# Attention with image prompts on one core: who sums the products of the last batch, and in which order its closing work runs

## The chip, the core and the metric

The kernel runs on one NeuronCore of a Trainium2 chip. A core has a matrix engine (PE, with weight loads shown apart as PEld), a vector engine (DVE), a scalar engine (ACT), a general engine (POOL, GpSimd) and a queue for transfers (SP). Each engine works through its own instructions in order and waits on semaphores for the others. The metric is the device time of one execution in microseconds (us). Three executions of the kernel before took 462.03, 462.84 and 463.11 us: a median of 462.84.

## What is computed

Eight batches (B) of 112 queries (S) with 320 channels, 20 heads of 16 channels, attend to 375 rows of context of width 512: 371 text rows and four image-prompt rows. The shapes of the inputs and the part of the reference that matters:

```python
q = heads(hidden_states @ W_q)
k_t = heads(text_ehs @ W_k)
v_t = heads(text_ehs @ W_v)
scores_t = jnp.einsum('bhsd,bhtd->bhst', q, k_t) * attn_scale
probs_t = jax.nn.softmax(scores_t, axis=-1)
text_out = jnp.einsum('bhst,bhtd->bhsd', probs_t, v_t)
k_ip = heads(ip_ehs @ W_k_ip)
v_ip = heads(ip_ehs @ W_v_ip)
attn_scores = jnp.einsum('bhsd,bhnd->bhsn', q, k_ip) * attn_scale
qsem = jnp.einsum('bhst,bte->bhse', probs_t, text_ehs)
qsem = _l2norm(qsem)
ip_n = _l2norm(ip_ehs)
sem = jnp.einsum('bhse,bne->bhsn', qsem, ip_n)
fused = attn_scores + SEM_SCALE * sem
probs_ip = jax.nn.softmax(fused, axis=-1)
probs_ip = probs_ip * spatial_mask[None, None, :, None]
ip_out = jnp.einsum('bhsn,bhnd->bhsd', probs_ip, v_ip)
out = text_out + IP_SCALE * ip_out
out = out @ W_out + b_out
out = out + residual
```

The norm of `qsem` needs, for every query and head, p G p', where p is a row of probabilities and G is the matrix of inner products of the text rows. The kernel computes it so, without forming `qsem`.

## The kernel before

All data are float32. The 20 heads of a batch go in five groups of four (`GROUP`, `NG`); a step (b, g) is one group of one batch, and 40 steps make the kernel. Batches are numbered 0 to 7, so "batch 7" is the last one and "the sixth" is b = 6.

**A step.** `scores` (L529 on, matmul L540) multiplies queries and keys of one head into a PSUM bank; `probabilities` takes the row maximum on DVE (L553), the exponential on ACT (L557) and sends the row by SP into a ring of two tiles (L560). This is done two steps ahead (`LEAD`). `transposed` turns the four heads' probabilities on DVE (L568). `multiplied` is the *product*: 96 matmuls on PE (L587) of the transposed probabilities with the tile `u`, which holds one triangle of G (off-diagonal parts doubled), the inner products with the four prompts, a column of ones and the values. Each of the four heads writes a bank of its own. `value_sums` copies the last 21 columns of each bank on ACT (L600). `reduced` multiplies the first 371 columns by the probabilities and sums them on DVE (L606) into `ss`; when the DVE and ACT have read a bank, the next product may write it. `placed` copies the next group's values into `u` on POOL (L506): three copies, each of which must wait until the running product has read that part of `u`.

**Banks.** PSUM has eight: four for the products (`ps_qd`), two for scores (`ps_sc`), two for everything else (`ps_mm`). In the last step of all, heads 0 and 1 use `ps_mm` banks.

**`finish(b)`** is a generator of pieces, each run by one call of `run(("f", b), ...)` or `next`: F1 (L640 to L647: `xb` on POOL, `z`, `rn` on DVE), F2 (L650: square root on ACT with a table load for it, then a table load for Exp; the scaled values `attn` on POOL, L656), F3 (L661 to L667: five small DVE operations up to `fu`), F4 (L671: Exp on ACT), F5 (L677 to L692: four small DVE operations up to `w`; then on POOL the product of prompt values and weights, L684, and three sums, L690 to L692), F6 (transposes on PE, L698; copy on ACT, L702), F7 (projection by `wo_sb` on PE, L711, six matmuls; bias and residual on DVE, L718) and F8 (the output's transfer on SP). In the last batch `finish` runs twice, once for heads 0 to 15 (`first`) and once for heads 16 to 19 (`last`, on DVE in place of POOL).

**Order.** PE, SP, DVE and ACT run in the order in which the code issues. POOL is ordered by the framework's planner, from a model of the times. In batches 0 to 6 `between(b, g)` puts the work for batch b + 1 between products: G in g = 0, `values` in g = 1 and 2, `keys` in g = 2 and 3. The keys come in three chunks of 128 channels; the last chunk holds 64 channels (heads 16 to 19) with gaps. For batches after the first its numbers are taken out of `values`: the weights `wv_sb` carry 64 more columns, the product is 384 wide in place of 320, POOL copies the additional columns to `k3` (L474), and PE transposes them (L439) in g = 3.

In the last batch nothing follows, so PE has only the five products, their scores, and what is left of `finish(6)` and `finish(7)`. Pieces of `finish(6)` lie so: F1 after product 0, F2 within product 1, F3 and F4 after it, F5 ahead of product 2, F6 after product 3, F7 and F8 among the first pieces of `first`. `awake` issues idle matmuls of the identity (L371).

Of the kernel before, what the change touches and what calls it, by code (L numbers as in the profile page):

```python
# [8 lines left out]
F32 = mybir.dt.float32  # L9
AF = mybir.ActivationFunctionType  # L10
ALU = mybir.AluOpType
# [9 lines left out]
def kernel(  # L21
# [60 lines left out]
    def bank(name, spare=False):  # L82

        if spare:
            return ps_sc.tile([P, 512], F32, tag="sc", name=name)
        return ps_mm.tile([P, 512], F32, tag="mm", name=name)
# [344 lines left out]
    def keys(b):  # L431
        s = st[b]
        for i in range(NC):
            ps = bank(f"ps_k_{b}_{i}")
            if b > 0 and i == FULL:

                for c in range(NT):
                    rows = min(P, TT - c * P)
                    nc.tensor.transpose(  # L439
                        ps[:, c * P : c * P + rows],  # L440
                        s["k3"][:rows, c].rearrange("p a r d -> p (a r d)"),
                        ident[:rows, :rows],
                    )
                nc.scalar.copy(s["kT"][:, i, :], ps[:, :TT])
                yield
                return
            for e in range(NE):
                nc.tensor.matmul(  # L448
                    ps[:, :TT],
                    wk_sb[:, e, i * P : (i + 1) * P],  # L450
                    s["ctxT"][:, e, :TT],
                    start=(e == 0),
                    stop=(e == NE - 1),
                )
            nc.scalar.copy(s["kT"][:, i, :], ps[:, :TT])  # L455
            yield

    def values(b):
        s = st[b]
        ctxT, vext = s["ctxT"], s["vext"]  # L460
        w = C if b == 0 else C + REST
        for c in range(NT):
            ps = bank(f"ps_v_{b}_{c}")
            for e in range(NE):
                nc.tensor.matmul(  # L465
                    ps[:, :w],
                    ctxT[:, e, c * P : (c + 1) * P],
                    wv_sb[:, e, :w],
                    start=(e == 0),
                    stop=(e == NE - 1),  # L470
                )
            nc.scalar.copy(vext[:, c, :w], ps[:, :w])  # L472
            if b > 0 and c == NT - 1:
                nc.gpsimd.tensor_copy(  # L474
                    s["k3"][:, :, :, 0, :],
                    vext[:, :, C:].rearrange("p c (a d) -> p c a d", d=D),
                )
            yield
# [31 lines left out]
    def prompt_logits(b):  # L510
        s = st[b]
        qT, _, j = queries[b]
        ps = bank(f"ps_ip_{b}")
        for i in range(NC):
            heads = slice(0, HC, 1) if i < FULL else slice(0, HC, 2)
            hn = min(HC, H - i * HC)
            nc.tensor.matmul(  # L517
                ps[:S, i * HC * NIP : (i * HC + hn) * NIP],
                qT[:, i, j * S : (j + 1) * S],
                kipb[:, i, b, heads, :],  # L520
                start=True,
                stop=True,
            )
        nc.scalar.copy(s["ipl"], ps[:S, :HN].rearrange("p (h n) -> p h n", n=NIP))
        yield
# [48 lines left out]
    def multiplied(b, g):  # L574
        s = st[b]
        xT = s.pop(("xT", g))
        banks = []
        for a in range(GROUP):

            if (b, g) == steps[-1] and a < 2:  # L580
                banks.append(bank(f"ps_qd_{b}_{g}_{a}"))
            else:
                banks.append(ps_qd.tile([P, 512], F32, tag="qd", name=f"ps_qd_{b}_{g}_{a}"))
        for j in range(BLK):
            c, q = j // QN, j % QN
            for a in range(GROUP):
                nc.tensor.matmul(  # L587
                    banks[a][:S, j * RG : UW],
                    xT[a * RG : (a + 1) * RG, j, :S],
                    region(b, c)[a * RG : (a + 1) * RG, q, q * RG :],  # L590
                    start=(j == 0),
                    stop=(j == BLK - 1),
                )
            yield
        s["qd", g] = banks
# [3 lines left out]
        for h, ps in zip(groups[g], s["qd", g]):  # L599
            nc.scalar.copy(s["pvs"][:, h, :], ps[:S, TT:UW])  # L600

    def reduced(b, g):
        s = st[b]
        for a, (h, ps) in enumerate(zip(groups[g], s.pop(("qd", g)))):
            junk = small.tile([S, TT], F32, tag="junk", name=f"junk_{b}_{h}", bufs=1)
            nc.vector.tensor_tensor_reduce(  # L606
                out=junk,
                in0=ps[:S, :TT],
                in1=s["p", g][:, a, :],
                scale=1.0,  # L610
                scalar=0.0,
                op0=ALU.mult,
                op1=ALU.add,
                accum_out=s["ss"][:, h : h + 1],
            )
        del s["p", g]


    def finish(b, heads=(0, H), eng=None, late=False, table=None):
# [14 lines left out]
        def over_ip(t):  # L634
            return t.unsqueeze(2).to_broadcast([S, n, NIP])
# [41 lines left out]
        nc.vector.tensor_reduce(sx, ex, AX.X, ALU.add)  # L677
        rx = sm("rx")
        nc.vector.reciprocal(rx, sx)
        nc.vector.tensor_scalar_mul(rx, rx, sm_sb)  # L680
        w = sm4("w")
        nc.vector.tensor_tensor(w, ex, over_ip(rx), ALU.mult)  # L682
        wv = work.tile([S, NIP, H, D], F32, tag="wv", name=f"wv_{b}_{h0}", bufs=1)[:, :, :n]
        eng.tensor_tensor(  # L684
            wv,
# [1 line left out]
            w.rearrange("p h n -> p n h").unsqueeze(3).to_broadcast([S, NIP, n, D]),  # L687
            ALU.mult,
        )
        eng.tensor_tensor(wv[:, :2], wv[:, :2], wv[:, 2:], ALU.add)  # L690
        eng.tensor_tensor(ah, ah, wv[:, 0], ALU.add)
        eng.tensor_tensor(ah, ah, wv[:, 1], ALU.add)  # L692
        yield

        i0, i1 = h0 * D // P, -(-h1 * D // P)
# [18 lines left out]
        if h1 < H:  # L714
            yield
            return
        ob = work.tile([S, C], F32, tag="ob", name=f"ob_{b}", bufs=1)
        nc.vector.tensor_tensor(ob, ps[:S, :C], s["xb"], ALU.add)  # L718
        yield
# [16 lines left out]
    def run(key, make, pieces=1):  # L736

        if key not in gens:
            gens[key] = make()
        for _ in range(pieces):  # L740
            next(gens[key], None)

    def between(b, g):
# [26 lines left out]
        if g == 3:  # L770
            if new:
                run(("k", nb), None, 1)
            for bs in first if b > 0 else ():
                run(("q", bs[0]), lambda: project_queries(bs), 3)
            run(("t", b), lambda: prompt_logits(b))
            if new:
                run(("k", nb), None, 1)
            if b > 0 and new:
                run(("f", b - 1), None)
            for bs in rest:  # L780
                run(("q", bs[0]), None)
        if g == 4:
            if nb + 1 < B:
                run(("c", nb + 1), lambda: transposed_context(nb + 1))
            if b > 0 and new:
                run(("f", b - 1), None)
            if nb + 1 < B:
                run(("c", nb + 1), None, 2)
            for bs in (first if b > 0 else []) + rest:
                run(("q", bs[0]), None)  # L790
# [87 lines left out]

    b = B - 1
    before = ("f", b - 1)
    for g in range(NG):
        coming = g + LEAD if g + LEAD < NG else None
        for a in (2, 3, 0, 1) if coming and g > 0 else ():
            scores(b, coming, a)
            probabilities(b, coming, a)
        if g == 2:
            run(before, None)
        for j, _ in enumerate(multiplied(b, g)):  # L890
            for a in {0: (2, 3), 1: (0, 1)}.get(j, ()) if g == 0 else ():
                scores(b, coming, a)
                probabilities(b, coming, a)
            if j == 2 and g + 1 < NG:
                transposed(b, g + 1)
            if j == 2 and g == 1:
                run(before, None)
        if g == 0:
            run(("f", b - 2), None)
        value_sums(b, g)  # L900
        reduced(b, g)
        if g + 1 < NG:
            placed(b, g + 1)
        if g == 1:
            prompt_values(b)
        between(b, g)
        if g == 1:
            run(before, None, 2)
        if g == 2:
            nc.scalar.preload_act_table(AF.Sqrt)  # L910
        if g == 3:
            run(before, None)

            first = finish(b, (0, FULL * HC), table=AF.Sqrt)
            for _ in range(4):
                next(first)
            run(before, None)
            next(first)
            run(before, None)
    last = finish(b, (FULL * HC, H), nc.vector, late=True)  # L920
    awake(16, end=True)
    for _ in range(4):
        next(last)
    next(first)
    next(first)
    drain(first)
    awake(3, end=True)
    drain(last)


# [41 lines left out]
```

## Time and profile before

| what | us |
|---|---|
| median of three executions | 462.84 |
| the profiled execution | 463.68 |
| its span, first to last instruction | 461.9 |
| PE busy / PEld busy | 444.7 / 341.1 |
| DVE busy | 317.0 |
| ACT busy | 183.7 |
| POOL busy | 108.0 |
| batch 6 (351 to 402): PE busy of 51.00 | 50.86 |
| batch 7 and the end (402 to 462): PE busy of 60.00 | 47.56 |

An engine's busy time is what its instructions took; a matmul that waits for a bank inside a pipelined run is still shown as busy, so a full PE row does not mean that it computes all the time. A row of the timeline gives start, duration, engine, line, operation, written and read tiles, shape, count, and in square brackets the idle time of the engine before it with what ended it. The granted clock of PE (PEclk) is 1.00 or 0.50, and stretches that mix the two lie between.

### The profile page before, as it was taken

The numbers are of one execution on the slowest core, as the hardware profiler recorded it, in microseconds if no ns is written. First come the engines' busy times: TensorE is split into PE (matmuls) and PEld (weight loads), VectorE is DVE, ScalarE is ACT, GpSimd is POOL, SyncE is SP. The second block draws the span as 40 slices with busy tenths as digits, with TensorE's granted clock in tenths as the row PEclk, the third lists the DMA queues.
The fourth block names the chain that finished last, engine by engine and source line by source line (L and its number), as shares of the span: only waits on it lengthen the run. The fifth ranks groups of instructions, "written<-read, shape, count | busy, mean of one in ns | idle before, by whom it ended". The sixth has DMA issues, their size and how long they took to land.

```text
span 461.9 us, 12998 instructions
## 1 busy us (share of the span) xinstructions
PE 444.7 (96%) x5147; PEld 341.1 (74%) x5147; DVE 317.0 (69%) x692; ACT 183.7 (40%) x505; POOL 108.0 (23%) x257
## 2 busy tenths in 40 slices
PE   8998999999999999999999999999999999999595
PEld 8757867787678877777678876787678877867373
DVE  3047466786768768786768768786768768798664
ACT  2263233345344443435344443435334434335131
POOL 4302200102051115111051115121051115011541
PEclk9999999999999999999999999999999999989798
DMA  8669954645655464546654464546654364544100
GB/s 254 168 163 255 201 156 108 152 125 160 164 137 132 141 170 129 131 128 174 166 134 130 144 170 128 128 134 173 170 133 125 86 175 121 132 139 124 44 14 12
DMA packets 52068, 64.99 MB, mean 141 GB/s; under 512 B 18368, under 2 KB 43984, under 8 KB 52008
## 3 DMA queue, kind: packets, MB, share of 16 engines
q1 hardware_dynamic: 51568, 63.62, 52.1%
q8 instruction: 40, 0.66, 0.6%
q10 hardware_dynamic: 440, 0.56, 0.4%
q14 instruction: 20, 0.16, 0.1%
HBM read 19.46 MB, written 5.12 MB: 53 GB/s over the span
## 4 chain that ended last, share of the span: by engine, by line
PE 91%; DVE 3%; ACT 2%; POOL 1%; DMA 1%; issue 1%; DVEq 0%
PE ps_qd L587 42%; PE ps_v L465 14%; PE ps_k L448 10%; PE ps_g L412 8%; PE ps_s L540 4%; PE ps_o L711 3%; PE ps_q L301 3%; PE ps_c L351 2%; PE ps_g L384 1%; DVE junk L606 1%; PE ps_k L439 1%; PE ps_ip L517 1%; ACT kT L455 1%; DVE xgT L568 1%; DMA ct<-in_ctx_dram 1%
## 5 line engine op out<-in xcount | busy, mean ns | idle before, releaser
L587 PE MATMUL ps_qd<-u,xgT 32*112 32x104 f32 (+11 forms) x3840 | 223.7, 357 | 7.5 <-POOL u L506 6.8
L587 PEld LDWEIGHTS ps_qd<-u,xgT 32*112 32x112 f32 x3840 | 185.5, 174 | 48.5 <-issue 11.9
L553 DVE TENSOR_REDUCE nmx<-ps_s 112x1 f32<-112x371 f32 x160 | 77.6, 529 | 70.0 <-PE ps_s L540 69.4
L568 DVE STREAM_TRANSPOSE xgT<-xg 128x1536 f32<-128x1536 f32 x40 | 118.8, 2970 | 5.5 <-DMA xg<-p 5.5
L557 ACT ACTIVATE p<-ps_s,nmx 112x371 f32<-112x371 f32 x160 | 82.5, 572 | 60.6 <-DVE nmx L553 51.1
L606 DVE CUSTOM_DVE_ANT_0 junk<-ps_qd,p 112x371 f32<-112x371 f32 x160 | 86.8, 542 | 25.5 <-ACT pvs L600 8.2
L506 POOL COPY u<-vr 128x64 f32<-128x64 f32 x120 | 26.0, 240 | 171.6 <-PE ps_qd L587 115.9
L465 PE MATMUL ps_v<-wv_sb,ctxT 128*128 128x384 f32 (+1 forms) x192 | 64.7, 487 | 0.0
L540 PE MATMUL ps_s<-kT,qm 32*112 32x371 f32 x320 | 63.0, 478 | 0.4 <-ACT p L557 0.4
L465 PEld LDWEIGHTS ps_v<-wv_sb,ctxT 128*128 128x128 f32 x192 | 35.2, 190 | 20.8
L600 ACT COPY pvs<-ps_qd 112x21 f32<-112x21 f32 x160 | 16.5, 189 | 80.2 <-PE ps_qd L587 80.1
L448 PE MATMUL ps_k<-ctxT,wk_sb 128*128 128x371 f32 x136 | 45.9, 482 | 0.0
L412 PE MATMUL ps_g<-ctxT 128*128 128x375 f32 (+2 forms) x168 | 37.4, 379 | 0.0
L448 PEld LDWEIGHTS ps_k<-ctxT,wk_sb 128*128 128x128 f32 x136 | 25.1, 190 | 15.4 <-issue 0.5
L412 PEld LDWEIGHTS ps_g<-ctxT 128*128 128x128 f32 x168 | 28.1, 190 | 8.4
L540 PEld LDWEIGHTS ps_s<-kT,qm 32*112 32x112 f32 x320 | 25.4, 170 | 4.6 <-ACT kT L455 2.0
L310 DVE TENSOR_SCALAR qm<-ps_q,emask 128x224 f32<-128x224 f32 (+1 forms) x25 | 9.2, 400 | 25.4 <-PE ps_q L301 25.4
L684 POOL TENSOR_TENSOR wv<-vip,w 112x1280 f32<-112x1280 f32 (+1 forms) x8 | 19.3, 2408 | 19.6 <-DVE w L682 19.6
L472 ACT COPY vext<-ps_v 128x384 f32<-128x384 f32 (+1 forms) x24 | 11.3, 472 | 27.5 <-PE ps_v L465 26.9
L455 ACT COPY kT<-ps_k 128x371 f32<-128x371 f32 x17 | 8.0, 469 | 27.5 <-PE ps_k L448 27.5
L400 ACT ACTIVATE ug<-ps_g 128x375 f32<-128x375 f32 (+2 forms) x24 | 9.0, 377 | 23.5 <-PE ps_g L412 20.5
L401 POOL TENSOR_TENSOR ug<-ug,half 128x128 f32<-128x128 f32 (+1 forms) x24 | 10.9, 457 | 29.9 <-ACT ug L400 29.9
(109 smaller groups left out, 317.3 us busy)
## 6 DMA issues: line engine op xcount, KB each, us to landing
xg<-p SPq DMA_DIRECT2D x160, 162.3 KB
u<-ug SPq DMA_DIRECT2D x128, 99.0 KB
vip<-vipd SPq DMA_DIRECT2D x8, 560.0 KB
ct<-in_ctx_dram SPq DMA_DIRECT2D x16, 256.0 KB
vr<-vd SPq DMA_DIRECT2D x32, 120.0 KB
vd<-vext SPq DMA_DIRECT2D x7, 320.0 KB
ct<-in_ctx_dram SPq DMA_DIRECT2D x8, 224.0 KB
vd<-vext SPq DMA_DIRECT2D x7, 160.0 KB
```

The costliest lines, as they stand in the source:

```text
L412: nc.tensor.matmul(ps[:, : T - t0], ctxT[:, e, t0 : t0 + P], ctxT[:, e, t0:T], start=(e == 0), stop=(e == NE - 1),)
L448: nc.tensor.matmul(ps[:, :TT], wk_sb[:, e, i * P : (i + 1) * P], s["ctxT"][:, e, :TT], start=(e == 0), stop=(e == NE - 1),)
L465: nc.tensor.matmul(ps[:, :w], ctxT[:, e, c * P : (c + 1) * P], wv_sb[:, e, :w], start=(e == 0), stop=(e == NE - 1),)
L506: nc.gpsimd.tensor_copy(region(b, c)[:, :, UV - c * P :], s["vr"][:, c * QN : (c + 1) * QN, g, :])
L540: nc.tensor.matmul(ps[:S, :TT], qm[a * RG : (a + 1) * RG, i, r, j * S : (j + 1) * S], s["kT"][a * RG : (a + 1) * RG, i, :], start=True, st ...
L553: nc.vector.tensor_reduce(nmx, ps[:S, :TT], AX.X, ALU.max, negate=True)
L557: nc.scalar.activation(p, ps[:S, :TT], AF.Exp, bias=nmx)
L568: nc.vector.transpose(xT.rearrange("p j (k q) -> p q j k", q=QN), xg.rearrange("p q (j k) -> p q j k", k=RG),)
L587: nc.tensor.matmul(banks[a][:S, j * RG : UW], xT[a * RG : (a + 1) * RG, j, :S], region(b, c)[a * RG : (a + 1) * RG, q, q * RG :], start=(j ...
L600: nc.scalar.copy(s["pvs"][:, h, :], ps[:S, TT:UW])
L606: nc.vector.tensor_tensor_reduce(out=junk, in0=ps[:S, :TT], in1=s["p", g][:, a, :], scale=1.0, scalar=0.0, op0=ALU.mult, op1=ALU.add, accu ...
L684: eng.tensor_tensor(wv, s["vip"][:, :, part], w.rearrange("p h n -> p n h").unsqueeze(3).to_broadcast([S, NIP, n, D]), ALU.mult,)
```

## The change

1. The square sums of heads 0 and 1 of steps g = 0, 1 and 2 of the last batch leave DVE. A new generator `shared` copies both banks to SBUF on ACT, multiplies by the probabilities on POOL, and sums with an accumulating ACT instruction that is issued in the following step (`drain(sums)`, ahead of the product). DVE's `reduced` starts at head 2 there.
2. The third chunk of the last batch's keys is made by a product of its own (four matmuls, each recorded as two) after product 1. The last batch's `values` are 320 wide, the copy to `k3` and the transposes in (6, 3) go.
3. Pieces of `finish(6)`: F2, F3 and F4 within product 1; F5 after product 2 (it was ahead of it); F6 and the projection after product 4 (they were ahead of it). F7 is split: the projection, then the addition of bias and residual, then the transfer.
4. Banks: in step 3 heads 0 and 1, in step 4 heads 2 and 3 use `ps_mm`. The last batch's prompt logits use a score bank.
5. The Sqrt table for the end is loaded ahead of product 3 and no longer after product 2. `first` runs five pieces in a row after product 3.
6. In F5 one DVE operation goes (the mask is folded into the one that follows), and `last` sums the prompts by one reduction and one addition in place of three additions. `awake` has 14 and 2 rounds in place of 16 and 3 (a round is two recorded matmuls).

```diff
-            if b > 0 and i == FULL:
+            if 0 < b < B - 1 and i == FULL:
...
-        w = C if b == 0 else C + REST
+        w = C + REST if 0 < b < B - 1 else C
...
-            if b > 0 and c == NT - 1:
+            if w > C and c == NT - 1:
...
-        ps = bank(f"ps_ip_{b}")
+        ps = bank(f"ps_ip_{b}", spare=b == B - 1)
...
-            if (b, g) == steps[-1] and a < 2:
+            if b == B - 1 and (g, a // 2) in ((NG - 2, 0), (NG - 1, 1)):
                 banks.append(bank(f"ps_qd_{b}_{g}_{a}"))
...
-    def reduced(b, g):
-        s = st[b]
-        for a, (h, ps) in enumerate(zip(groups[g], s.pop(("qd", g)))):
+    def shared(b, g):
+
+        s = st[b]
+        some = list(enumerate(zip(groups[g], s["qd", g])))[:2]
+        t = work.tile([P, NE, TP], F32, tag="ctxT", name=f"shared_{b}_{g}")
+        prods = [t[:S, a, :TT] for a, _ in some]
+        p = s["p", g]
+        for a, (h, ps) in some:
+            nc.scalar.copy(prods[a], ps[:S, :TT])
+        yield
+
+        for a, _ in some:
+            nc.gpsimd.tensor_tensor(prods[a], prods[a], p[:, a, :], ALU.mult)
+        yield
+
+        for a, (h, _) in some:
+            nc.scalar.activation(prods[a], prods[a], AF.Copy, accum_out=s["ss"][:, h : h + 1])
+        yield
+
+    def reduced(b, g, a0=0):
+        s = st[b]
+        for a, (h, ps) in list(enumerate(zip(groups[g], s.pop(("qd", g)))))[a0:]:
...
-        nc.vector.tensor_scalar_mul(rx, rx, sm_sb)
         w = sm4("w")
-        nc.vector.tensor_tensor(w, ex, over_ip(rx), ALU.mult)
+        nc.vector.scalar_tensor_tensor(w, ex, sm_sb, over_ip(rx), ALU.mult, ALU.mult)
...
-        eng.tensor_tensor(wv[:, :2], wv[:, :2], wv[:, 2:], ALU.add)
-        eng.tensor_tensor(ah, ah, wv[:, 0], ALU.add)
-        eng.tensor_tensor(ah, ah, wv[:, 1], ALU.add)
+        if late:
+            ips = small.tile([S, GROUP, D], F32, tag="ips", name=f"ips_{b}", bufs=1)
+            nc.vector.tensor_reduce(ips, wv.rearrange("p n h d -> p h d n"), AX.X, ALU.add)
+            nc.vector.tensor_tensor(ah, ah, ips, ALU.add)
+        else:
+            eng.tensor_tensor(wv[:, :2], wv[:, :2], wv[:, 2:], ALU.add)
+            eng.tensor_tensor(ah, ah, wv[:, 0], ALU.add)
+            eng.tensor_tensor(ah, ah, wv[:, 1], ALU.add)
...
         if h1 < H:
             yield
             return
+        yield
+
         ob = work.tile([S, C], F32, tag="ob", name=f"ob_{b}", bufs=1)
...
-            if new:
+            if nb < B - 1:
                 run(("k", nb), None, 1)
...
             if b > 0 and new:
-                run(("f", b - 1), None)
+                run(("f", b - 1), None, 2)
...
     before = ("f", b - 1)
+    sums = iter(())
     for g in range(NG):
...
-        if g == 2:
-            run(before, None)
+        drain(sums)
+        if g == 3:
+            nc.scalar.preload_act_table(AF.Sqrt)
...
             if j == 2 and g == 1:
-                run(before, None)
+                run(before, None, 3)
+        value_sums(b, g)
+        if g < LEAD + 1:
+            sums = shared(b, g)
+            next(sums)
+            reduced(b, g, 2)
+        else:
+            reduced(b, g)
+        if g + 1 < NG:
+            placed(b, g + 1)
+        if g < LEAD + 1:
+            next(sums)
         if g == 0:
             run(("f", b - 2), None)
-        value_sums(b, g)
-        reduced(b, g)
-        if g + 1 < NG:
-            placed(b, g + 1)
         if g == 1:
             prompt_values(b)
+            run(("k", b), None)
         between(b, g)
-        if g == 1:
-            run(before, None, 2)
         if g == 2:
-            nc.scalar.preload_act_table(AF.Sqrt)
+            run(before, None)
         if g == 3:
-            run(before, None)
 
             first = finish(b, (0, FULL * HC), table=AF.Sqrt)
-            for _ in range(4):
+            for _ in range(5):
                 next(first)
-            run(before, None)
-            next(first)
-            run(before, None)
     last = finish(b, (FULL * HC, H), nc.vector, late=True)
-    awake(16, end=True)
-    for _ in range(4):
+    run(before, None, 2)
+    awake(14, end=True)
+    for _ in range(3):
         next(last)
+    run(before, None)
+    next(last)
     next(first)
     next(first)
+    run(before, None)
     drain(first)
-    awake(3, end=True)
+    awake(2, end=True)
     drain(last)
```

## The prediction, made before the changed kernel was run

> **What bounds the kernel now.** I read the page first: PE is busy 444.7 of 461.9 us, and up to 403 us its row has no hole, so there only PE's own work counts. Then the timeline of each engine over batch 7. There PE waits ahead of every product. The products' rows:
>
> ```profile
> 411.14 8.20 PE L587 MATMUL ps_qd<-u,xgT 32*112 32x392 f32 x93 [0.58 <-DVE ss L606]
> 420.40 6.78 PE L587 MATMUL ps_qd<-u,xgT 32*112 32x392 f32 x96
> 432.78 6.96 PE L587 MATMUL ps_qd<-u,xgT 32*112 32x392 f32 x96 [5.60 <-POOL u L506]
> 443.09 4.80 PE L587 MATMUL ps_qd<-u,xgT 32*112 32x392 f32 x96
> ```
>
> The same 96 matmuls take 4.80 us in product 4 and up to 8.20 elsewhere. In 1 and 2 the first four matmuls wait one by one for DVE's sums to free the banks: by the weight loads, all four are free at 413.13 and 422.39. Product 3 waits 5.6 us for POOL, whose queue is this:
>
> ```profile
> 426.58 2.47 POOL L684 TENSOR_TENSOR wv<-vip,w 112x1280 f32<-112x1280 f32 x1 [6.61 <-DVE w L682]
> 429.13 1.54 POOL L690 TENSOR_TENSOR wv<-wv 112x640 f32<-112x640 f32 x1
> 430.75 0.86 POOL L691 TENSOR_TENSOR attn<-attn,wv 112x320 f32<-112x320 f32 x1
> 431.68 0.86 POOL L692 TENSOR_TENSOR attn<-attn,wv 112x320 f32<-112x320 f32 x1
> 432.49 0.58 POOL L506 COPY u<-vr 128x64 f32<-128x64 f32 x3
> ```
>
> The rest is the clock. Stretches of 3.41 us, laid so that every change of the granted clock falls on an edge (columns: PE, PEld, DVE, ACT and POOL busy, PEclk, DMA share, GB/s):
>
> ```profile
> 409.89:413.30 3.41, 2.83 (x18) 1.02 (x15) 2.94 (x11) 0.32 (x4) 0.24 (x1) 1.00 0.51 145
> 413.30:416.71 3.41, 3.41 (x28) 2.65 (x30) 3.38 (x7) 2.56 (x5) 0.00 (x0) 0.50 0.12 30
> 420.13:423.54 3.41, 3.31 (x25) 1.66 (x26) 2.84 (x13) 0.00 (x0) 0.00 (x0) 1.00 0.40 129
> 423.54:426.95 3.41, 3.41 (x80) 3.28 (x74) 3.23 (x10) 2.23 (x5) 0.36 (x1) 1.00 0.17 45
> 426.95:430.37 3.42, 0.23 (x3) 0.11 (x2) 3.28 (x4) 1.70 (x5) 3.34 (x2) 1.00 0.54 152
> 430.37:433.78 3.41, 1.00 (x8) 0.68 (x12) 3.12 (x7) 0.00 (x0) 2.54 (x6) 0.50 0.00 0
> ```
>
> A stretch with 1.02 us of weight loads is followed by half clock, one with 1.66 is not. So PE need not be idle for a whole stretch: losing about half of one suffices, and costs 1.7 us (half of the next).
>
> **The changes, in the trace's own clock.** *Batch 6.* `values` at 384 columns: 16 matmuls in 5.36 us in the chain of waits, 0.335 each; at 320, estimated in proportion, 0.279. 24 matmuls save 1.34. The three transposes save 0.51 (chain, 394.20). PE is the bound there (50.86 of 51.00 busy) and the next products' banks and `u` are ready 0.9 us or more before PE comes, so all **1.85** counts.
>
> *Product 1.* DVE comes late to the sums of product 0 (410.45, after its transpose) and needs 0.70 for each head. New: after `value_sums` (ends 410.21) ACT copies heads 0 and 1; the nearest row, the copy of `kT` (371 columns, 469 ns), gives 410.68 and 411.10. DVE's two heads end at 411.75. Product 1 then runs from 411.75 instead of 413.13 with only 1.2 us lost, so with no cold stretch, and ends at 416.45 (4.7 us, as product 2 from 422.39) instead of 419.6. That is 3.1 us, and ACT gives most of it back. ACT's queue before:
>
> ```profile
> 414.13 1.95 ACT L557 ACTIVATE p<-ps_s,nmx 112x371 f32<-112x371 f32 x4 [3.92 <-DVE nmx L553]
> 416.10 1.28 ACT L650 ACT_TABLE_LOAD   x1
> 417.40 0.22 ACT L650 ACTIVATE rn<-rn 112x20 f32<-112x20 f32 x1
> 417.63 1.28 ACT L651 ACT_TABLE_LOAD   x1
> 419.49 0.41 ACT L600 COPY pvs<-ps_qd 112x21 f32<-112x21 f32 x4 [0.57 <-PE ps_qd L587]
> ```
>
> The exponentials end 1.39 earlier (two heads fewer on DVE): 414.69. Then come two accumulating ACT instructions, an operation that this trace does not have. Bounds: 0.4 (the copy alone) and 1.0 each (twice the exponential's 0.49); I take 0.52, by the exponential's row. 415.75. Two table loads and the root: 418.53; F3 on DVE, 1.37 after the root (its five operations, 422.26 to 423.63): 418.64; Exp 0.27: 418.93. Only now `value_sums` of product 1, 419.34, two copies, 420.25, the new `kT` copy, 420.70. Meanwhile PE does the own product of the keys, 8 recorded matmuls by the 2.7 us that 8 such took at 390.86: 416.45 to 419.15, **hidden** in PE's wait for ACT (without that cover it would cost 2.7). Scores of step 4 (8 in 1.1 us) then run 420.75 to 421.85, and product 2 starts: 421.85 against 422.39. It ends at 426.6 against 427.1.
>
> Behind the accumulating instructions stand, on ACT, the table loads and all of the above: each additional 0.1 us of one costs 0.2 here. In steps 2 and 3 ACT has 1.9 and 0.8 us of slack ahead of `value_sums`.
>
> *Product 3.* F5 now comes after `placed(3)`. Banks of heads 0 and 1 are the free `ps_mm` ones; those of 2 and 3 need ACT's copies: 426.6 + 0.1 + 0.41 + 2 x 0.45 = 428.0. `u` is complete at 427.2, the transposed tile (DVE, scores at 421 on, four maxima, 2.9) at 426. Start 428.0 in place of 432.78, warm (1.1 us lost): end **432.8** in place of 439.67.
>
> *Product 4.* What is late next is POOL again, one step on. It multiplies heads 0 and 1: width 371 lies between the rows 112x320 (0.86) and 112x640 (1.55), so 0.97 each, 427.55 to 429.5. Then F5's chain; its `w` is ready at 429.15 (DVE: two heads to 428.3, three small operations). 5.95 us as above: 435.45. `placed(4)` follows, by the order that POOL kept before (426.58 to 432.49): 436.05. Banks are free by 435.0, the logits end at 433.55, F6 and F7 no longer stand here (2.4 us with their wait). Start 436.1 in place of 443.09. But PE has then been idle 2.5 us, and most positions of a 3.41 us stretch hold enough of that: 1.6 us of cold clock. End 436.1 + 4.8 + 1.6 = **442.5** against 447.93, which is 5.4 earlier.
>
> *The end,* counted from product 4's. Before: 461.9 - 447.93 = 13.97. New, on PE: transposes, `value_sums` and copy 1.0; projection 1.87, now here; 28 idle matmuls at 0.12, 3.36; two transposes 0.4, ACT's copy 0.35, projection 4 x 0.31 now warm, 4 idle ones 0.48: 8.73. DVE's chain for the last four heads is ready at 7.4 (7.85 before, less 0.34 for the dropped operation and 0.1 for the reduction) and waits for PE. Transpose, copy, two matmuls, addition, transfer as before but warm: 1.65 + 2.98. Sum 13.36, so 0.6 better. DVE's addition for batch 6 fits into the 0.5 us in which DVE waits for Exp; POOL's `xb` has 3 us.
>
> **Sum:** 1.85 + 5.4 + 0.6 = 7.9 us of the span of 461.9. The profiled execution took 463.68, 0.8 over the median; the gain is taken off the median: 462.84 - 7.9 = **454.9, say 455.0**.
>
> **Two rules against the rows.** The Trainium skill, "TensorE: Matmul & The Clock Gate", section "HAM oscillation", warns of idle gaps beyond about 3.4 us. By it the 2.5 us ahead of product 4 would be free and the time 453.4; the row 409.89 (clock halved after a stretch that PE still worked in) says otherwise and I follow it. The 3.41 us spacing itself agrees with that page. "GPSIMD Engine Reference", section "Engine selection", advises VectorE over GpSimd for elementwise work, about twice as slow with two inputs. By it the move loses: 0.70 on DVE becomes 0.45 + 0.97 + 0.52 on two engines. Three steps, if all stood on the path, would lose 6 x 1.24 = 7.4 us. In the rows the bank is free after the first 0.45, and the other parts find POOL and ACT idle except where I charged them.
>
> **Rivals.**
> (a) Cold also at product 2. PE waits 1.65 us there before the scores; a stretch that holds all of it is on the edge between the two rows. Another 1.7: 456.7. 22%.
> (b) No cold stretch at product 4: the window falls well (453.4), or the planner puts `placed(4)` ahead of F5's chain, so that the product starts at 434.4 (451.7). Against it: POOL took the chain first before. 24%.
> (c) The planner puts the two POOL multiplications of step 2 behind F5's chain. They end at 437.05, ACT's sums, the Sqrt load and `value_sums` follow to 439.8, DVE's two heads to 441.0; product 4 starts there, cold: 460.1. Against it: the copies are ready before `w`. 7%.
> (d) Slower: the accumulating instruction is dear. Six of them stand in ACT's queue in steps 1 to 3, with 1.9 and 0.8 us of slack. At x us each the loss is 6(x - 0.52) - 2.7, and equals the whole gain at x = 2.3; at 3.0 the time is 467. No row is near such a price. 3%.
>
> My forecast has 40%; 4% is left for what I do not see. The range 451.2 to 458.2 takes in (a), (b) and accumulating instructions at their upper bound (1 us on top of (a)), and leaves out (c) and (d). A difference under 0.2% (0.9 us) cannot be told from none with runs that lie 1.1 us apart. Faster 95%, no change 2%, slower 3%.
>
> **What would show it.** Product 1 about 4.7 us long, with no half clock behind product 0; ACT's `value_sums` of product 1 idle-free behind Exp of F4; product 3 about 1.4 us after product 2; product 4 waiting for POOL's L506 behind F5's sums; half clock in it; and PE, not DVE, last at the end. I am wrong if ACT's sums exceed 1 us, if POOL's order differs, or if batch 6 does not shorten by 1.85.

## The result, and the profile after

The changed kernel takes 456.19 us (median of four, 455.51 to 457.10) against 462.98 for the kernel before on the same chip: a ratio of 0.9857, interval 0.983 to 0.9883. 455.0 was forecast. The profiled execution took 457.10 us, with a span of 455.3.

The four executions come in two pairs, 455.51 and 455.67 at a mean granted clock of 0.996 and 0.995, 456.71 and 457.10 at 0.991. One stretch of 3.41 us at half clock lowers the mean over 455 us by 3.41 / 2 / 455 = 0.0037, about the difference of the pairs. The forecast had one such stretch in the last batch; its rival (a), at 456.7, had two. By their mean clock two of the four executions have one and two have two. Only the profiled one, the longest of the four, left a trace; it has two.

The products of the last batch on PE, in the timeline of the changed kernel:

```profile
408.75 5.78 PE L587 MATMUL ps_qd<-u,xgT 32*112 32x392 f32 x96 [0.19 <-DVE xgT L568]
414.46 2.76 PE L448 MATMUL ps_k<-ctxT,wk_sb 128*128 128x371 f32 x8
420.12 12.10 PE L587 MATMUL ps_qd<-u,xgT 32*112 32x392 f32 x192
435.61 6.49 PE L587 MATMUL ps_qd<-u,xgT 32*112 32x392 f32 x96 [2.70 <-POOL u L506]
```

Product 1 lasts 5.78 us where it took 8.20, with the own product of the keys (L448) behind it. Products 2 and 3 merge into one row: what was a gap of 5.6 us between them is some 1 us, from product 2's end at 426.5 to 427.6, when ACT has copied the last bank. The wait for POOL's L506 has moved to product 4, 2.70 us long, and that product takes 6.49 us where 4.80 would do.

POOL around it, in the same kernel:

```profile
427.32 1.91 POOL L614 TENSOR_TENSOR shared<-shared,p 112x371 f32<-112x371 f32 x2 [0.40 <-ACT shared L610]
429.41 2.47 POOL L702 TENSOR_TENSOR wv<-vip,w 112x1280 f32<-112x1280 f32 x1 [0.17 <-DVE w L700]
431.95 1.55 POOL L713 TENSOR_TENSOR wv<-wv 112x640 f32<-112x640 f32 x1
433.58 0.86 POOL L714 TENSOR_TENSOR attn<-attn,wv 112x320 f32<-112x320 f32 x1
434.52 0.86 POOL L715 TENSOR_TENSOR attn<-attn,wv 112x320 f32<-112x320 f32 x1
435.32 0.61 POOL L506 COPY u<-vr 128x64 f32<-128x64 f32 x3
```

The two multiplications, F5's product and its three sums run without a pause, and only then come the copies for which product 4 waits.

The clock, again in stretches laid on its edges (same columns as above):

```profile
413.13:416.55 3.42, 3.42 (x47) 2.64 (x43) 3.11 (x4) 3.37 (x8) 0.67 (x1) 1.00 0.56 155
416.55:419.96 3.41, 1.32 (x11) 0.55 (x13) 2.00 (x8) 2.48 (x9) 2.08 (x6) 1.00 0.73 215
419.96:423.37 3.41, 3.41 (x28) 1.93 (x24) 3.01 (x5) 2.39 (x7) 0.54 (x1) 0.50 0.08 17
433.61:437.03 3.42, 1.42 (x20) 0.93 (x24) 2.93 (x11) 1.15 (x2) 2.87 (x6) 0.99 0.02 5
437.03:440.44 3.41, 3.41 (x36) 2.48 (x32) 1.28 (x6) 1.89 (x3) 1.40 (x1) 0.50 0.00 0
```

Half clock follows the stretches in which PE is busy for 1.32 and 1.42 us: the waits before product 2 and before product 4. PE is idle there for 2.09 us (417.22 to 419.31) and for 2.70: neither wait is as long as a stretch.

ACT in step 1, from the exponentials to `value_sums` of product 1, with the accumulating instructions (L618), an operation that the kernel before does not have (the dots stand for two table loads and the square root):

```profile
411.58 1.96 ACT L557 ACTIVATE p<-ps_s,nmx 112x371 f32<-112x371 f32 x4 [2.61 <-POOL shared L614]
413.40 0.53 ACT L618 ACTIVATE shared<-shared 112x371 f32<-112x371 f32 x1
413.81 0.22 ACT L618 ACTIVATION_READ_ACCUMULATOR shared<-shared 112x1 f32 x1
413.90 0.53 ACT L618 ACTIVATE shared<-shared 112x371 f32<-112x371 f32 x1
414.30 0.21 ACT L618 ACTIVATION_READ_ACCUMULATOR shared<-shared 112x1 f32 x1
...
417.58 0.27 ACT L690 ACTIVATE ex<-fu 112x80 f32<-112x80 f32 x1 [0.23 <-DVE fu L686]
417.76 0.39 ACT L600 COPY pvs<-ps_qd 112x21 f32<-112x21 f32 x4
```

### The profile page after: what moved, and what is told of

The parts are those of the page before. It is cut to its first block, busy times and chain, and to the rows that moved or that the text cites. A ratio compares the mean times of both kernels' runs of the same rounds, so it can differ in the third digit from the quotient of the medians.

```text
span 455.3 us, 12992 instructions
## 1 busy us (share of the span) xinstructions
PE 440.5 (97%) x5146; PEld 340.1 (75%) x5146; DVE 313.7 (69%) x670; ACT 188.8 (41%) x523; POOL 113.3 (25%) x262
## 5 line engine op out<-in xcount | busy, mean ns | idle before, releaser
L587 PE MATMUL ps_qd<-u,xgT 32*112 32x232 f32 (+11 forms) x3840 | 220.9, 356 | 4.2 <-POOL u L506 3.8
L625 DVE CUSTOM_DVE_ANT_0 junk<-ps_qd,p 112x371 f32<-112x371 f32 x154 | 83.5, 542 | 22.5 <-ACT pvs L600 5.7
L506 POOL COPY u<-vr 128x64 f32<-128x64 f32 x120 | 26.1, 240 | 169.4 <-PE ps_qd L587 113.4
L465 PE MATMUL ps_v<-wv_sb,ctxT 128*128 128x384 f32 (+1 forms) x192 | 63.5, 480 | 0.0
L448 PE MATMUL ps_k<-ctxT,wk_sb 128*128 128x371 f32 x144 | 48.7, 482 | 0.0
L448 PEld LDWEIGHTS ps_k<-ctxT,wk_sb 128*128 128x128 f32 x144 | 26.5, 190 | 16.1 <-issue 0.5
L702 POOL TENSOR_TENSOR wv<-vip,w 112x1280 f32<-112x1280 f32 (+1 forms) x8 | 19.2, 2405 | 17.0 <-DVE w L700 14.8
L472 ACT COPY vext<-ps_v 128x384 f32<-128x384 f32 (+1 forms) x24 | 11.2, 466 | 24.9 <-PE ps_v L465 24.4
```

Source lines behind the costliest of these rows:

```text
L448: nc.tensor.matmul(ps[:, :TT], wk_sb[:, e, i * P : (i + 1) * P], s["ctxT"][:, e, :TT], start=(e == 0), stop=(e == NE - 1),)
L465: nc.tensor.matmul(ps[:, :w], ctxT[:, e, c * P : (c + 1) * P], wv_sb[:, e, :w], start=(e == 0), stop=(e == NE - 1),)
L506: nc.gpsimd.tensor_copy(region(b, c)[:, :, UV - c * P :], s["vr"][:, c * QN : (c + 1) * QN, g, :])
L587: nc.tensor.matmul(banks[a][:S, j * RG : UW], xT[a * RG : (a + 1) * RG, j, :S], region(b, c)[a * RG : (a + 1) * RG, q, q * RG :], start=(j ...
L625: nc.vector.tensor_tensor_reduce(out=junk, in0=ps[:S, :TT], in1=s["p", g][:, a, :], scale=1.0, scalar=0.0, op0=ALU.mult, op1=ALU.add, accu ...
L702: eng.tensor_tensor(wv, s["vip"][:, :, part], w.rearrange("p h n -> p n h").unsqueeze(3).to_broadcast([S, NIP, n, D]), ALU.mult,)
```

## Experiments

All medians below are of four to six executions, each group beside the kernel before on the same chip. "Changed kernel" is the one above. The half-clock times in this table are read from the granted clock of the one profiled execution in quarter-microsecond steps, from 398 us to the last output. A median is taken over executions that can have one stretch more or less, and by the intervals a median is good to about 1 us.

| kernel | median us | ratio to before, interval | half clock while PE computes, us |
|---|---|---|---|
| kernel before | 462.98 | 1 | 413.3-416.8, 430.3-437.3, 454.3-457.8 |
| changed kernel | 456.19 | 0.9857 [0.983, 0.9883] | 419.8-423.5, 437.0-440.5 |
| sums_dve | 457.73 | 0.9893 [0.9869, 0.9918] | 436.0-439.8 |
| keys_values | 459.42 | 0.9929 [0.9903, 0.9955] | 418.8-425.8, 435.8-442.8 |
| f5_ahead | 457.75 | 0.9897 [0.9868, 0.9925] | 419.0-422.8, 429.3-433.0 |
| proj_back | 459.64 | 0.9926 [0.9902, 0.9951] | 419.3-423.0, 436.5-440.0, 450.0-453.8 |
| warm | 453.89 | 0.9796 [0.9773, 0.9819] | none |
| f1_later | 454.16 | 0.9806 [0.9784, 0.9828] | 432.3-435.8 |
| placed_first | 455.43 | 0.9825 [0.9798, 0.9851] | 419.5-423.0 |
| all | 452.86 | 0.9776 [0.9755, 0.9798] | none |
| all2 | 452.64 | 0.9776 [0.9757, 0.9795] | none |
| keys_values_warm | 455.00 | 0.9821 [0.9801, 0.9842] | none |
| f1_warm | 453.21 | 0.9784 [0.9766, 0.9802] | none |

The kernel before has more half clock than the changed one. A run of it with idle matmuls in its waits was not made, so how much of the 6.8 us could be had without the change is open.

### One part undone at a time

**sums_dve**: all four sums of each step on DVE.

```diff
-        if g < LEAD + 1:
-            sums = shared(b, g)
-            next(sums)
-            reduced(b, g, 2)
-        else:
-            reduced(b, g)
+        reduced(b, g)
...
-        if g < LEAD + 1:
-            next(sums)
```

> All four sums of every step of the last batch on DVE again, the rest as in the changed kernel (456.2 us). Theory (ACT's queue in step 1 gives back what the early banks bring): product 1 starts 1.4 us later, but ACT loses two copies and two sums, so product 2 ends within 0.8 us of where it does now; in step 2 the two further sums hold F5's weights back and product 4 starts 1.2 us later. 457.3, between 456.5 and 458.5. Rival (the early banks are the main gain): three steps each lose 1.2 us or more, 459.2 or above.

457.73, within the theory's range. The part with the most new instructions, six heads' sums on two other engines, is worth 1.5 us. The first half of the theory is in the trace: counted from product 0, product 1 ends 1.4 us later than in the changed kernel, and product 2 still ends no later, as ACT has no copies of banks ahead of the new keys and no half clock falls into product 2. The second half is not: product 4 starts 0.3 us later, and not 1.2. But the two traces are unlike executions, the fastest of six here (457.04) and the longest of four there (457.10), with one stretch of half clock against two. Where the 1.5 us of the medians lie, they do not show.

**keys_values**: the last batch's third chunk of keys from its values, as in the other batches.

```diff
-        w = C + REST if 0 < b < B - 1 else C
+        w = C if b == 0 else C + REST
...
-            if nb < B - 1:
+            if new:
                 run(("k", nb), None, 1)
...
-            run(("k", b), None)
```

> The last batch's third chunk of keys out of its values again (384 wide, copy to k3, transposes in batch 6), no own product after product 1. Theory (the own product lies in PE's wait for ACT): batch 6 loses 1.9 to 2.0 us, product 2 gains 1.0 since its scores need no new keys: 457.2, between 456.5 and 458.5, with PE idle some 3.8 us ahead of product 2 and half clock behind it. Rival (the own product's 2.7 us are on the path): 455.5.

459.42, outside both. The wait and the half clock behind it are the expected ones, and the size is not. Products 2 and 4 in its timeline on PE:

```profile
420.57 8.12 PE L587 MATMUL ps_qd<-u,xgT 32*112 32x392 f32 x100 [3.46 <-ACT shared L610]
437.27 7.48 PE L587 MATMUL ps_qd<-u,xgT 32*112 32x392 f32 x96 [2.68 <-POOL u L506]
```

PE is idle for 3.46 us ahead of product 2 where it had worked on keys, and 8.12 us for little more than one product means half clock over nearly all of it: 7 us of it in the table, twice. I had allowed for one stretch of 3.4. Whether that is the whole difference was asked with idle matmuls in those places (keys_values_warm, below).

**f5_ahead**: F5 of batch 6 ahead of product 2.

```diff
         drain(sums)
+        if g == 2:
+            run(before, None)
...
-        if g == 2:
-            run(before, None)
```

> F5 of batch 6 ahead of product 2 again, the rest as in the changed kernel. Theory (moving F5 only moves PE's wait for POOL one step on): product 3 waits some 3 us for POOL's L506 behind F5's chain and runs partly cold, product 4 waits for neither; 456.5, between 455.5 and 457.5. Rival (the 5.6 us wait before product 3 was removed by this move): 459.5 to 461.

457.75, 0.25 above the theory's bound and 1.75 below the rival's. Its products 3 and 4:

```profile
429.55 6.46 PE L587 MATMUL ps_qd<-u,xgT 32*112 32x392 f32 x96 [3.40 <-POOL u L506]
436.63 5.65 PE L587 MATMUL ps_qd<-u,xgT 32*112 32x392 f32 x96
```

The wait for POOL is back at product 3, with 3.40 us, and gone at product 4, which ends at 442.3, where the changed kernel has 442.1. So the move of F5 took away no wait; it put the wait one step on. The profiled executions differ by 1.1 us of the medians' 1.6, and 0.9 of that lies in the end, 14.1 us long in place of 13.2: product 3 ends later without the move, and POOL begins the last batch's own closing work (L675) at 439.6 in place of 436.1.

**proj_back**: F6 and the projection of batch 6 ahead of product 4.

```diff
         if g == 3:
+            run(before, None)
             first = finish(b, (0, FULL * HC), table=AF.Sqrt)
-            for _ in range(5):
+            for _ in range(4):
                 next(first)
+            run(before, None, 2)
+            next(first)
+            run(before, None)
...
-    run(before, None, 2)
     awake(14, end=True)
```

> F6 and the projection of batch 6 ahead of product 4 again, the rest as in the changed kernel. Theory: they need F5's sums on POOL, which end at the same moment as the wait of product 4, so product 4 starts 2.5 to 2.7 us later; the end gets 1.3 shorter, as PE no longer is the last there; and PE works through part of the wait, which may save the cold stretch (1.4): 457.0, between 456.0 and 458.0. Rival (they lay in a wait that is there anyway): 454.9.

459.64, above the theory by 1.6 and on the other side of its rival. Three rows of PE:

```profile
436.28 3.31 PE L734 MATMUL ps_o<-wo_sb,aT 128*112 128x320 f32 x6 [0.53 <-ACT aT L725]
439.52 4.99 PE L587 MATMUL ps_qd<-u,xgT 32*112 32x392 f32 x96
449.92 2.23 PE L734 MATMUL ps_o<-wo_sb,aT 128*112 128x320 f32 x4 [1.89 <-ACT aT L725]
```

The projection itself falls into half clock, 3.31 us for the 1.87 that it takes at the end of the changed kernel, so product 4 starts at 439.5 and not at 438.3. And with the projection gone from the end, PE runs dry there for 1.89 us: the last batch's first projection takes 2.23 us in place of 1.33. The 1.3 us that I expected from a shorter end are eaten by that. Moved behind product 4, the six matmuls no longer hold it up, and no half clock falls into the end. proj_back with idle matmuls in its waits was not tried.

### The clock: idle matmuls in PE's waits

**warm** adds only work, 36 matmuls of the identity:

```diff
             run(("k", b), None)
+            awake(8)
...
         if g == 3:
+            awake(10)
```

> The changed kernel (456.2 us) with idle matmuls of the identity in PE's two longest waits: 16 after the own product of the keys, 20 after the prompt logits. Theory (half clock behind these waits costs up to 1.35 us in product 2 and 1.65 us in product 4): both products take 4.8 to 5.0 us, no half clock between 400 us and the last transfer, 453.9, between 453.2 and 454.8. Rival (the waits themselves are the loss, the clock is not): 456.2, unchanged, or slower by matmuls that stand in the way.

453.89 where 453.9 was expected; its executions lie between 453.03 and 454.09, so that close a hit is luck. In its timeline PE's rows are

```profile
417.25 1.95 PE L371 MATMUL ps_w<-ident 128*128 128x128 f32 x16
420.20 4.71 PE L587 MATMUL ps_qd<-u,xgT 32*112 32x392 f32 x96
431.24 2.48 PE L371 MATMUL ps_w<-ident 128*128 128x128 f32 x20
434.10 4.80 PE L587 MATMUL ps_qd<-u,xgT 32*112 32x392 f32 x96 [0.39 <-POOL u L506]
```

Product 2 still waits for ACT and product 4 for POOL, now behind idle matmuls; both take 4.7 to 4.8 us. The waits are still there: product 2 starts 11.2 us after product 1, in the changed kernel 11.4. So the clock behind them was worth 2.3 us of the median of 456.2, and 3.2 between the profiled executions (457.10 and 453.91), where the changed kernel has both stretches.

**keys_values_warm**: keys_values with `awake(11)` after product 1 and `awake(10)` after the logits.

> Kernel keys_values (459.4 us) with 22 idle matmuls after product 1 and 20 after the prompt logits. Theory (what the own product of the keys is worth beyond the 0.7 us that batch 6 gives on balance is the clock it keeps): no half clock in products 2 and 4, 454.7 against 453.9 of kernel warm, between 454.0 and 455.5. Rival (scores and sums without the own product lie badly): 456.5 or above.

455.00, within the theory: keys_values lay 3.2 us above the changed kernel; with the clock kept up in both, 1.1 are left (455.00 against 453.89 of warm). The own product does not save work. It moves 1.98 us out of a batch in which PE is the bound into a wait, and it keeps PE busy there.

### The late value_sums: DVE held by POOL

ACT reached `value_sums` of product 1 later than forecast (below). The row that stood out was DVE's first piece for batch 6:

```profile
409.61 1.00 DVE L661 COPY z<-pvs 112x20 f32<-112x20 f32 x1
```

In the kernel before, the same copy took 0.17 us:

```profile
413.00 0.17 DVE L642 COPY z<-pvs 112x20 f32<-112x20 f32 x1
```

The 1.00 us end at 410.6, when POOL's multiplication of heads 0 and 1 ends:

```profile
408.68 1.90 POOL L614 TENSOR_TENSOR shared<-shared,p 112x371 f32<-112x371 f32 x2 [0.43 <-ACT shared L610]
```

sums_dve has no such multiplication and has the copy in the same place of DVE's queue. There it takes 0.17 us:

```profile
410.62 0.17 DVE L661 COPY z<-pvs 112x20 f32<-112x20 f32 x1
```

**f1_later** issues the piece behind the four maxima:

```diff
-            if b > 0:
+            if 0 < b < B - 1:
                 run(("f", b - 1), lambda: finish(b - 1))
...
+        if g == 1:
+            run(before, lambda: finish(b - 1))
         drain(sums)
```

> The changed kernel with the first piece of batch 6's closing work (z, z2, rn on DVE) behind the four maxima of step 1, so that it no longer meets POOL's multiplication. Theory (DVE's copy of z took 1.00 us, elsewhere 0.17, because POOL works on SBUF at that time, and this delays everything in ACT's queue): z takes 0.17 to 0.25, ACT's value_sums of product 1 and the scores of step 4 come 0.8 us earlier; 455.2, between 454.3 and 455.9, part of it by fewer cold stretches. Rival (the 0.8 us are lost in a wait for something else): 456.2.

454.16, 0.1 better than the theory's bound. DVE and ACT in its timeline:

```profile
409.06 1.89 DVE L553 TENSOR_REDUCE nmx<-ps_s 112x1 f32<-112x371 f32 x4
410.87 0.17 DVE L661 COPY z<-pvs 112x20 f32<-112x20 f32 x1
```

```profile
410.06 1.95 ACT L557 ACTIVATE p<-ps_s,nmx 112x371 f32<-112x371 f32 x4 [1.65 <-POOL shared L614]
416.45 0.39 ACT L600 COPY pvs<-ps_qd 112x21 f32<-112x21 f32 x4
```

The copy takes 0.17 us again. Counted from the start of product 1 (408.21 here, 408.75 in the changed kernel), `value_sums` comes after 8.24 us in place of 9.01: 0.8 earlier. Not all of this need be the hold. The move also takes the piece's own 0.5 us from ahead of the maxima, and the exponentials now start when POOL's multiplication ends (ACT's row names L614), so the two are not told apart by this run. PE's wait ahead of the scores for product 2 is 1.3 us in place of 2.1, and no half clock follows:

```profile
418.73 4.71 PE L587 MATMUL ps_qd<-u,xgT 32*112 32x392 f32 x96
```

### POOL's order, and a better version

**placed_first** orders POOL by hand in the last batch: the copies for product 4 lie between F5's product and its sums, and `xb` of the last batch is issued at the end.

```diff
+    engines = engines | {mybir.EngineType.Activation, mybir.EngineType.Pool}
+    ctx.enter_context(tc.manual_schedule(engines=engines))
...
             placed(b, g + 1)
+        if g == 3:
+            run(before, None)
...
             ALU.mult,
         )
+        yield
+
         if late:
```

> The changed kernel with POOL ordered by hand in the last batch: the copies into u for product 4 go between F5's product of prompt values and its three sums; xb of the last batch is issued at its end. Theory (product 4 waits for POOL's order alone): it starts 2.0 us earlier, limited by DVE's sums of heads 0 and 1, PE waits 1.0 us in place of 3.0 and product 4 keeps full clock (1.65 us more); the end is not longer, since POOL's last sums come at the same moment. 453.0, between 452.2 and 454.0. Rival (the end then waits for POOL's sums of the last batch, which do not come earlier): 455.5 or above.

455.43: half of each. Product 4 ends 3.3 us earlier than in the changed kernel (438.8 against 442.1), as the theory had it. But from there to the end it takes 14.8 us in place of 13.2. The hand order has a cost in step 1 too: POOL's `xb` of batch 6 now runs right behind the multiplication (410.64 to 411.50), DVE's second small operation (L665) ends with it at 411.53, and `value_sums` of product 1 comes 0.9 us later, counted from product 0. **all** joins the hand order, the later first piece and `awake(5)` after the keys.

> Hand order of POOL, the later first piece, and 10 idle matmuls after the own product of the keys, together. Theory (the three gains add up): from the level of two cold stretches, 457.0, less 0.8, 1.35 and 3.65: 451.2, between 450.4 and 452.4, with no half clock before the last transfer. Rival (they overlap: the end becomes the bound by POOL's sums of the last batch): 453 or above.

452.86, between the theory's bound (452.4) and the rival's (453): without any half clock the same 14.8 us stand at the end (product 4 ends at 436.2 of a span of 451.0). Two causes offered themselves. ACT loads the Sqrt table until 437.3 and so comes 1.1 us late to `value_sums`; or DVE's operations for the last four heads are held up by POOL. ACT in all:

```profile
436.05 1.28 ACT L693 ACT_TABLE_LOAD   x1
437.34 0.41 ACT L600 COPY pvs<-ps_qd 112x21 f32<-112x21 f32 x4
```

**all2** takes the load out of the way:

```diff
-            first = finish(b, (0, FULL * HC), table=AF.Sqrt)
+            first = finish(b, (0, FULL * HC))
...
+    nc.scalar.preload_act_table(AF.Sqrt)
     awake(14, end=True)
```

> Kernel all (452.9 us) with the last Sqrt table load moved from behind Exp of heads 0 to 15 to behind the copy of batch 6's aT, after product 4. Theory (with product 4 earlier, ACT's table load of 1.28 us stands between it and value_sums, 1.1 us): value_sums starts at the end of product 4, 451.8, between 451.4 and 452.2. Rival (the end is bound by DVE operations that POOL's sums hold up, z, rn and attn of the last four heads): they are held up as long or longer, 452.5 or above.

452.64, within the spread of all (452.55 to 453.01): the rival. The lines of ACT, DVE and POOL in the timeline of all2:

```profile
436.37 0.41 ACT L600 COPY pvs<-ps_qd 112x21 f32<-112x21 f32 x4
```

```profile
439.67 1.04 DVE L662 COPY z<-pvs 112x4 f32<-112x4 f32 x1
...
440.94 0.58 DVE L667 TENSOR_TENSOR rn<-ss,z 112x4 f32<-112x4 f32 x1
441.44 0.17 DVE L673 RECIPROCAL zr<-z 112x4 f32<-112x4 f32 x1
441.64 0.74 DVE L676 TENSOR_TENSOR attn<-pvs,zr 112x64 f32<-112x64 f32 x1
```

```profile
439.42 1.27 POOL L716 TENSOR_TENSOR wv<-wv 112x512 f32<-112x512 f32 x1
440.77 0.74 POOL L717 TENSOR_TENSOR attn<-attn,wv 112x256 f32<-112x256 f32 x1
441.58 0.73 POOL L718 TENSOR_TENSOR attn<-attn,wv 112x256 f32<-112x256 f32 x1
```

`value_sums` is on time, DVE comes to the last four heads 0.7 us sooner after product 4's start than in all, and there a copy of four columns takes 0.9 us more than the 0.16 of the changed kernel and ends with POOL's addition; `rn` and `attn` end with the next two. What ACT gained, DVE lost. By the chain of work that ended last, these DVE operations lead to the end of the kernel. A version in which POOL and DVE do not meet at the end was not tried.

**f1_warm** is f1_later with `awake(5)` and `awake(10)`, POOL in the planner's order.

> Kernel f1_later with 10 idle matmuls after the own product and 20 after the prompt logits, POOL in the planner's order. Theory (POOL's order is worth a wait of 2 us less before product 4, of which the end takes back most): 453.1 to 453.4, that is 0.3 to 0.6 above kernel all. Rival (hand order is worth its 2 us): 454.5 or above.

453.21, as the theory had it: without a hand order, and 0.35 us above all. Idle matmuls and one moved piece are worth 3.0 us; the hand order of POOL is worth next to nothing on top. all2, at 0.9776 of the kernel before, has the lowest median of those tried, but its executions (452.44 to 453.57) cannot be told from those of all or of f1_warm (452.75 to 453.49).

## Why the prediction was right, and where it was not

The median fell to 456.19 where 455.0 was forecast, well inside the range. Part of that nearness is luck: the forecast counted one stretch of half clock, and half of the executions have two. The profiled execution's span fell by 461.9 - 455.3 = 6.6 us; the sum of the forecast was 7.9. By its own steps (starts and ends in the clock of the kernel before, which means 1.98 us added to those of the changed one):

| step | forecast | measured |
|---|---|---|
| batch 6 and product 0 earlier | 1.85 | 1.98 (401.43 against 403.41) |
| product 1 ends | 416.45 | 416.4 |
| value_sums of product 1 start | 418.93 | 419.74 |
| product 2 starts | 421.85 | 422.1 |
| half clock in product 2 | rival (a) | yes, 1.6 us |
| product 2 ends | 426.6 | 428.4 |
| product 4 starts | 436.1 | 437.6 |
| half clock in product 4 | 1.6 us | 6.49 for 4.80, 1.7 us |
| product 4 ends | 442.5 | 444.1 |
| from there to the end | 13.36 | 13.2 |

The half clock in product 2 is the term that is missing: 6.3 us from its start to ACT's `value_sums` (420.12 to 426.46), where f1_later takes 4.7 (418.73 to 423.46). Its late end goes on to POOL's multiplications (429.3 for the forecast 427.55), through F5's chain to product 4, and so to the end.

- **Batch 6, product 1, the own product in PE's wait:** right, to 0.15 us.
- **ACT's queue in step 1:** right as the bound, 0.8 us too short. The term that failed is DVE's: "The exponentials end 1.39 earlier". They end 0.56 earlier (413.54, with 1.98 added 415.52, against 416.08). F1 lies ahead of the maxima, and its copy was held until POOL's multiplication ended (0.83 us more than its row). sums_dve shows the copy unheld without the multiplication; in f1_later, with the piece moved, the 0.8 us are gone. The accumulating instruction, for which no row existed, was right: the pair takes 1.1 us (413.40 to 414.51) where 2 x 0.52 was taken.
- **The clock:** right about product 4; the wait before product 2 was put at 1.65 us and was 2.1 by that delay, and rival (a), held to be half as likely as the forecast, came in two of four executions. warm shows what both stretches together cost. The rule of 3.4 us of idle time, weighed in the prediction, would have seen neither. But the prediction's own measure, weight loads, does not hold in the later traces: on the same grid of stretches, full clock followed one with 1.04 us of loads in f1_later (415.27 to 418.69, PE busy for 2.08), and half clock one with 1.95 in keys_values (432.49 to 435.90, PE busy for 2.10).
- **POOL as the next wait, behind F5's chain:** right in place and order, and in the size of the wait (2.70 us where 2.5 was taken). placed_first and f5_ahead show it from two sides. Rival (b), the copies ahead of that chain or no half clock at product 4, did not happen in the profiled execution.
- **The end:** right in sum, with the projection of batch 6 in it (PE's terms as written add to 8.70 and not to 8.73, which changes nothing). It was only worked out for the order that the change has; in proj_back and placed_first, where I shifted pieces of it, I was off by 1.4 and 1.6 us, once by PE running dry and the half clock behind it, once by POOL holding DVE (all2).
- **Rival (d)**, a dear accumulating instruction, and rival (c), the multiplications behind F5's chain, did not happen; the rows of ACT and POOL in the result show it.

What the part undone alone brings back (1.5, 3.2, 1.6 and 3.4 us) sums to 9.7, more than the 6.8 gained: the parts are not independent. For one of them, keys_values, it is shown that 2.1 of its 3.2 us are half clock; for the others it was not taken apart.

## What to carry to other kernels

When a change shortens a wait, ask how much of a 3.4 us stretch PE still works, and fill it: real work that was elsewhere on the path is best (1.1 us better here), idle matmuls do as well for the clock. When work moves from DVE to POOL, look for DVE's small operations that fall into POOL's: they cost POOL's remaining time, not their own. Here a piece moved off one wait brought the same engine's wait one step later; work out what is late next before counting the gain.

## What the runs showed of the hardware

- POOL's operations on SBUF hold up some of DVE's, and end them together. In all2 a copy of four columns took 1.04 us in place of 0.16, an operation with two inputs in SBUF (L667) 0.58 in place of 0.16. Others were not held: in all2 the sums that read PSUM beside POOL's L703 (0.54 each, as elsewhere); in the changed kernel a reciprocal beside L614 (0.28 at 428.26, and 0.28 at 425.61 in the kernel before with POOL idle) and the 32 x 32 transposes beside L702 and L713 (2.99 at 429.25, and 2.92 at 415.32 in the kernel before with POOL idle). The Trainium skill, "GPSIMD Engine Reference", section "Specifications", says that the SBUF interface is shared with VectorE, with contention for DVE instructions in a 2-port mode or with two inputs in SBUF; these rows agree for the operations with two inputs; which mode the copies run in no run here shows. The profile of the kernel before had it already, on an operation that takes 0.16 us in the changed kernel, and I read past it:

```profile
451.12 0.58 DVE L647 TENSOR_TENSOR rn<-ss,z 112x4 f32<-112x4 f32 x1
```

```profile
450.94 0.74 POOL L692 TENSOR_TENSOR attn<-attn,wv 112x256 f32<-112x256 f32 x1
```

  Both end at about 451.7.
- Half clock followed stretches of 3.41 us in which PE was busy for 1.32 and 1.42 us, and, in the kernel before, one in which it was shown busy for 2.83 with 1.02 of weight loads. The time shown busy does not settle it alone: full clock followed 2.08 us in f1_later, half clock 2.10 us in keys_values. What decides between them was not measured.
